# Four-layer convolutional network on one Trainium2 core: image additions moved to GpSimd and fills, stores and products reordered at two job boundaries

## The chip, the core and the metric

The kernel runs on one NeuronCore of a Trainium2 chip. The core has a matrix engine (TensorE, "PE" in the profile; its weight loads are listed apart as "PEld"), three engines for elementwise work (VectorE "DVE", ScalarE "ACT", GpSimd "POOL"), and SyncE ("SP"), which here only issues transfers. Each engine works through its own instructions in the order in which they were recorded, and waits on semaphores for the others. A transfer (DMA) is issued from a queue: SyncE's and ScalarE's go through a hardware queue each (q1 and q10 in the profile), GpSimd's through a software queue (q0). Matrix products are accumulated in PSUM banks; everything else lives in on-chip SBUF tiles or in DRAM.

The metric is the device time of one execution in microseconds (us), lower is better. One execution of each kernel is also recorded by the profiler; its trace starts at 0 and its length is called the span.

## What is computed

An image of 1024 channels by 64 x 64 pixels (4096 tokens) goes through four layers, each normalized in 32 groups and added back to its input:

```python
x = x + _L0_conv_ref(_gn(x), ...)   # decayed cumulative sum over the channels
x = x + _L1_conv_ref(_gn(x), ...)   # 1x1 convolution: einsum('oi,nihw->nohw', weight, x) + bias
x = x + _L2_conv_ref(_gn(x), ...)   # in_proj (three parts), scan over a permuted token order, out_proj
x = x + _L3_conv_ref(_gn(x), ...)   # 1x1 convolution + bias
return x
...
# the end of layer 2
y = y * jax.nn.silu(gate) + res
return jax.nn.silu(jnp.einsum('oc,bchw->bohw', out_proj_w, y) + out_proj_b[None, :, None, None])
...
def _gn(v, G=32, eps=1e-5):
    g = v.reshape(B_, G, C_ // G, H_, W_)
    m = jnp.mean(g, axis=(2, 3, 4), keepdims=True)
    s = jnp.var(g, axis=(2, 3, 4), keepdims=True)
    return ((g - m) / jnp.sqrt(s + eps)).reshape(v.shape)
```

Every large part is a 1024 x 1024 matrix times a 1024 x 4096 image. Layer 3 can only start once layer 2's whole output is known, since its normalization needs the mean and variance of each group of channels over all 4096 pixels. A group lies inside one block of 128 channels, so that the upper 512 channels (row 0) and the lower 512 (row 1) can be normalized one after the other.

## The kernel before

**Jobs.** The last 1070 us of the span belong to `two_steps` (line 1514). It works through twelve jobs: for each of four pairs of 512-pixel column blocks a "gate" job (third part of in_proj) and an "out" job (out_proj), then four "last" jobs (layer 3). Jobs are counted from 0: job 7 is the last out_proj job, job 8 the first of layer 3 (`turning`). Each job multiplies a 1024 x 1024 matrix by a 1024 x 1024 piece of the image with Strassen's scheme (in Winograd's form) applied twice. On the outer level the piece is four tiles b11, b12 (row 0, left and right columns) and b21, b22 (row 1), each 128 partitions x 4 sub-tiles (k = 0 to 3) x 512 columns, and four sums of them:

- t1 = b12 - b11, t2 = b22 - t1, t3 = t2 - b11, t4 = b21 - t2.

There are seven outer products, P1 (b11), P2 (b21), P3 (b22), P4 (t4), P5 (t1), P6 (t2), P7 (t3), and inside each the same seven again, on quarters of the outer operand. I write P5P2 for the inner product P2 of the outer product P5. The 49 products of a job are 8 matmuls each (128 x 256 columns), with a weight tile of 256 KB that SyncE loads ten tiles ahead (`wq`). P1P1, P1P2 and P1P3 read quarters of b11 itself: P1P1 its sub-tiles k = 0, 1, the other two k = 2, 3. P1P6, P1P7, P1P5 and P1P4 read the inner sums t2, t3, t1 and t4 of b11, which `inner_sum` (line 1547 is the subtraction) makes on GpSimd.

**Where work stands.** `plan(j)` puts every other instruction of a job at a slot: `then(slot, f)` appends it to `at[slot]`; a slot stands behind one product. The loop at the end of `two_steps` goes through the slots: first the product, then the slot's list in the order in which it was planned. So what an engine does, and in which order, is fixed by hand. Products of two outer products are interleaved: even places of a slot group of seven take P1, P2, P6, P7 of the current outer product, odd places P5, P4, P3 of the one before. At the first slots of job 8 a table (`instead`) puts the three leftovers of job 7 first.

**The names that matter here.**

- `fetch` (L1544) loads a 1 MB tile (`x_x_b11` and so on, or the image `x_x_D`, `x_x_Q`, `x_x_V` that is added back) on ScalarE's queue; `fill` (L1551) normalizes one sub-tile on ScalarE into `qb`; `comb` makes an outer sum (t1 overwrites b12, by `alias`) on VectorE, through the same line 1547.
- `emit` empties a product's PSUM bank: a "put" into a fresh tile is a ScalarE copy (L1752), anything else a VectorE sum (L1754 to L1763). A later product that adds onto the same bank waits for that.
- The out_proj job has four result tiles, C, D, Q and V, each 128 x 4 x 512. In job 7 (`final`, so `quick`) each sub-tile takes silu (L1715, ScalarE), the addition of the image (L1717, VectorE), and `quarter_stats` (L1590, VectorE bn_stats); then `keep` (L1729) stores the tile to `x2_d` on ScalarE's queue.
- `next_norm` makes layer 3's normalization, for row 0 from slot 44 of job 7 and for row 1 from slot 56 (that is slot 7 of job 8): `gn_mv` (L183, the statistics summed on VectorE), the small matmul `pg` (L200), `gn_d` (L203 to L205, VectorE), the small matmul `pv` (L209), `gn_v`, then logarithm and exponential on ScalarE (L170, L171) and four VectorE steps to `gn_bias` (L220). The ScalarE functions logarithm and silu need different tables: a table load stands where it changes (L1598, and at L1715).
- At the start of job 0 the last results of the stage before are still coming: `activate` (L1095 silu, L1097 store to `res_d`) empties the list `silus`; before the loop ends this is called with GpSimd as the issuing queue, and two tiles (`rg`) are left for it.

Of the kernel before, what the change touches and what calls it, by code (L numbers as in the profile page):

```python
# [15 lines left out]
ALU = mybir.AluOpType  # L16
# [78 lines left out]
def tile_net(ctx: ExitStack, tc: tile.TileContext, x, par_d, cst_d, w_d, w2_d, dbcw_d, out):  # L95
# [1266 lines left out]
    with tc.tile_pool(name="l2g", bufs=8) as pgat, tc.tile_pool(name="l2b", bufs=2) as pb, tc.tile_pool(name="l2r2", bufs=4) as prg, tc.tile_pool(name="l2h", bufs=1) as ph, \  # L1362
# [87 lines left out]
        with tc.manual_schedule(engines={E_.DVE, E_.PE, E_.Pool, E_.Activation}):  # L1450
            for k in range(5):
                gather(k)
            while given < first:
                next_units(total)
                if len(silus) > 3:
                    activate(4)
            step_sums(0)
            for k in range(-1, NK + 1):
                upto = first + (k + 2) * (total - first) // (NK + 2)
                if 4 < k + 5 < NK:  # L1460
                    gather(k + 5)
                turned = turn_rows(k + 1) if k + 1 < NK else None
                if k > 0:
                    weigh(k - 1, pgs.pop(k - 1))
                if turned is not None:
                    spread_decay(k + 1, *turned)
                if k + 2 < NK:
                    step_sums(k + 2)
                next_units(upto)
                y = apply(k - 1) if k > 0 else None  # L1470
                if 0 <= k < NK:
                    pgs[k] = cross(k)
                if k + 1 < NK:
                    nc.scalar.activation(decay_[k + 1], decay_[k + 1], AF.Exp)
                if y is not None:
                    scatter(k - 1, y)
                next_units(upto)
                if given // 2 % 14 != 12:
                    next(sums, None)
                if len(silus) > 3:  # L1480
                    activate(4)
            while given < total:
                next_units(total)
            next(units, None)
            while silus:
                activate(4, nc.gpsimd)
            for _ in sums:
                pass
    rg_pool.__exit__(None, None, None)
# [24 lines left out]
    def two_steps(jobs, norm2):  # L1514
# [3 lines left out]
        orders = [ORDER_B if kind == "out" else ORDER_A for kind in kinds]  # L1518
        orders[turning - 1 : turning + 1] = ORDER_C, ORDER_D
        norm3 = {}  # L1520
        at = {}
        held = {}
        inner = {}
        bank = {}
# [66 lines left out]

        def next_norm(s0):

            for row, slot, after, last in ((0, 44, (4, 4, 5, 5), 5), (1, 56, (3, 3, 4, 4), 5)):
                steps = {}

                def begin(row=row, steps=steps):
# [13 lines left out]
        def plan(j):  # L1611
# [6 lines left out]
            def on(slot, f, *a):  # L1618
                then(s0 + slot, lambda: f(*a))


            if kind != "out":
                for name, row, col, slot, when in (
                        (("b11", 0, 0, -7, 1), ("b12", 0, 1, -3, 2), ("b21", 1, 0, 6, 12), ("b22", 1, 1, 8, 14))
                        if order is ORDER_D else
                        (("b11", 0, 0, -25, -14), ("b12", 0, 1, -14, -3), ("b21", 1, 0, -10, -1), ("b22", 1, 1, 1, 8))):
                    on(slot, fetch, src_d, pair, row, col, (j, "x", name))
                    for k in range(KH):
                        on(when + (k // 2 if when in (1, 12) and order is ORDER_D else k), fill, j, name, row, col, k)
                late = [(1, "t1", "b12", "b11"), (9, "t2", "b22", "t1"), (13, "t3", "t2", "b11"), (27, "t4", "b21", "t2")]  # L1630
                ks = [range(KH)] * 4
                put_in = {2: 12}
# [6 lines left out]
                put_in = {1: 4, 3: 19}  # L1639
            if order is ORDER_C:  # L1640
                late[3] = (32, *late[3][1:])
            for (slot, to, a, b), kk in zip(late, ks):
                for i, k in enumerate(kk):
                    on(slot + i, comb, j, to, a, b, k)

            def alias(to, old):
                held[j, to] = tile_of(j, old)
            at[s0 + late[0][0]].insert(0, lambda: alias("t1", "b12"))
            at[s0 + late[2][0]].insert(0, lambda: alias("t3", "b11"))
            if order is not ORDER_D:  # L1650
                at[s0 + late[3][0]].insert(0, lambda: alias("t4", "b22" if order is ORDER_C else "t2"))
# [49 lines left out]
            for name, row, col, when in done:  # L1701
# [4 lines left out]
                for k, slot in when.items():  # L1706
                    o = row * KH + k

                    def one(name=name, nb=nb, row=row, k=k, o=o):
# [4 lines left out]
                            return  # L1714
                        nc.scalar.activation(c, c, AF.Silu, bias=pcol("bout", o))  # L1715
                        if quick:
                            nc.vector.tensor_tensor(c, c, held[j, "x", name][:, k], ALU.add)  # L1717
                            quarter_stats(tile_of(j, name), row, nb, k)
                    on(slot, one)
                    if kind == "last":  # L1720
# [12 lines left out]
                if not quick:  # L1733
# [3 lines left out]
                            on(when[k + 1] + 10 + i, lambda name=name, row=row, nb=nb, k=k + i: quarter_stats(  # L1737
                                tile_of(j, name), row, nb, k))
                    end += 11
                on(end + 1, keep)  # L1740
            if kind == "out" and final:
                next_norm(s0)

# [21 lines left out]
        def product(j, outer, name):  # L1765
# [15 lines left out]
            for o in range(OG):  # L1781
                for k in range(2):
                    nc.tensor.matmul(ps[:, o, :], w[:, k, o * P : (o + 1) * P], rhs[:, k, :],  # L1783
                                     start=(new and o == 0 and k == 0), stop=(k == 1), skip_group_check=True)
            for kind, row, col in {"P1": [("put", 0, 0)], "P2": [("add", 0, 0)], "P6": [("put", 1, 0)],
                                   "P7": [("put", 1, 1)], "P5": [("put", 0, 1), ("add", 1, 1)],
                                   "P4": [("add", 1, 0)], "P3": [("add", 0, 1)]}[name]:
                emit(j, outer, kind, row, col, ps)

        for j in range(len(jobs)):  # L1790
            plan(j)
        end = len(jobs) * JOB
# [3 lines left out]
        for slot in range(min(at), max(max(at), end + 6) + 1):  # L1796
# [3 lines left out]
            if 0 <= step < 7 * len(jobs):  # L1800
                j, s = divmod(step, 7)
                outer = orders[j][s]
                product(j, outer, ("P1", "P5", "P2", "P4", "P6", "P3", "P7")[i])
            for f in at.get(slot, ()):
                f()

    with tc.manual_schedule(engines={E_.DVE, E_.PE, E_.Pool, E_.Activation}):
# [101 lines left out]
```

## Time and profile before

| | |
|---|---|
| time, median of 3 runs | 2644.04 us |
| fastest, slowest of them | 2640.99, 2644.49 us |
| the profiled execution | 2645.31 us |
| its span | 2643.2 us |
| granted TensorE clock, mean | 0.994 of full |
| TensorE busy | 2559.3 us (97%) |
| VectorE, GpSimd, ScalarE busy | 1818.2 (69%), 1212.4 (46%), 1057.0 (40%) |
| moved by DMA | 597.22 MB, mean 226 GB/s |

Busy time is the sum over an engine's instructions. With TensorE at 97% of the span, what another engine does counts only where TensorE waits for it. In timelines a line reads: start, length, engine, source line, operation, output from inputs, shapes, count, and in brackets how long the engine was idle before it and what ended that. In the chain of waits each line is a piece of work that the next one had to wait for. Line numbers are those of the kernel before; in the kernel after, lines up to 1617 keep their numbers and later ones stand 6 to 13 lines further down (the matmuls of the products at L1793, the image addition at L1727).

### The profile page before, as it was taken

Reading aid. Unit: us, or ns where it says so; the run is one execution under the profiler, and the core shown is the slowest. Engines: PE = TensorE matmul, PEld = TensorE weight load, DVE = VectorE, ACT = ScalarE, POOL = GpSimd, SP = SyncE. Lnnn points to the kernel's source line nnn. Section 1 sums busy time; section 2 is a strip of 40 time slices with the busy share of each in tenths; the row PEclk is TensorE's granted clock in tenths of the full one; section 3 lists DMA queues with packets and bytes.
Section 4 is the critical chain, followed back from the end, with each engine's and each line's share of the span. In section 5 each row is a group of like instructions: output and inputs, shape, how many; then the busy total and the mean of one; then the engine's idle time right before and its main releaser. Section 6 shows DMA issues by size and latency. Waiting matters only on the chain.

```text
span 2643.2 us, 30741 instructions
## 1 busy us (share of the span) xinstructions
PE 2559.3 (97%) x9588; PEld 1712.5 (65%) x9588; DVE 1818.2 (69%) x3782; ACT 1057.0 (40%) x1799; POOL 1212.4 (46%) x1098
## 2 busy tenths in 40 slices
PE   5889999999999999999999999999999999899999
PEld 5764444444555445544454558888888888788887
DVE  7987675665564554377877766576585775877877
ACT  4672010005655644476867662233233322312120
POOL 2553223322414241256464645566565755554544
PEclk9999999999999999999999999999999999999999
DMA  6565648655655676577677847899898898888896
GB/s 253 189 211 170 232 137 284 209 158 189 196 147 139 151 193 158 178 248 224 206 241 241 282 140 209 223 281 290 237 298 254 240 303 224 277 287 301 301 320 216
DMA packets 426868, 597.22 MB, mean 226 GB/s; under 512 B 142004, under 2 KB 210739, under 8 KB 423636
## 3 DMA queue, kind: packets, MB, share of 16 engines
q1 hardware_dynamic: 307268, 384.68, 46.1%
q10 hardware_dynamic: 91456, 136.33, 14.7%
q0 software_dynamic: 27984, 74.26, 11.8%
q8 instruction: 78, 1.28, 0.2%
q14 instruction: 82, 0.67, 0.1%
HBM read 435.10 MB, written 160.05 MB: 225 GB/s over the span
## 4 chain that ended last, share of the span: by engine, by line
PE 83%; DVE 9%; ACT 5%; issue 1%; DMA 1%; POOL 1%; SPq 0%; DVEq 0%; POOLq 0%; ACTq 0%
PE mm L892 37%; PE q_P2P L1783 6%; PE q_P6P L1783 5%; PE q_P5P L1783 5%; PE q_P3P L1783 5%; PE q_P7P L1783 5%; PE q_P4P L1783 5%; PE q_P1P L1783 5%; PE py L1430 2%; PE l2pt L1145 2%; DVE xt L658 1%; DVE cvp L1126 1%; ACT b L996 1%; PE pd L623 1%; DVE stats L567 1%
## 5 line engine op out<-in xcount | busy, mean ns | idle before, releaser
L892 PE MATMUL mm<-t,w 128*128 128x512 f32 x1536 | 681.1, 594 | 0.0
L892 PE MATMUL mm<-b,w 128*128 128x512 f32 x1152 | 512.7, 596 | 5.0 <-ACT b L996 3.9
L892 PEld LDWEIGHTS mm<-t,w 128*128 128x128 f32 x1536 | 285.8, 190 | 321.3 <-issue 314.3
L892 PEld LDWEIGHTS mm<-b,w 128*128 128x128 f32 x1152 | 215.3, 191 | 252.0 <-issue 239.1
L1439 POOL DMA_INDIRECT y_rows<-g,dst x74 | 74.1, 1002 | 185.0 <-ACT g L1435 171.3
L1126 DVE SCALAR_TENSOR_TENSOR cvp<-xs,par,cvp 128x512 f32<-128x512 f32 x128 | 95.3, 753 | 76.8 <-ACT cvp L1123 74.5
L1752 ACT COPY qQ<-q_P5P 128x512 f32<-128x512 f32 x48 | 28.1, 585 | 292.0 <-PE q_P5P L1783 292.0
L470 POOL TENSOR_TENSOR s<-s 128x256 f32<-128x256 f32 (+3 forms) x120 | 130.3, 1091 | 7.5
L1433 ACT COPY g<-py 8x512 f32<-8x512 f32 x146 | 83.8, 574 | 107.5 <-PE py L1430 103.3
L1177 DVE TENSOR_TENSOR xs<-mm,xs 128x512 f32<-128x512 f32 x64 | 41.8, 685 | 116.1 <-PE mm L892 116.1
L1153 POOL TENSOR_TENSOR acc<-l2xt,acc 128x136 f32<-128x136 f32 x56 | 27.8, 497 | 194.4 <-ACT l2xt L1147 187.3
L1013 DVE SCALAR_TENSOR_TENSOR image<-mm,par,image 128x512 f32<-128x512 f32 x64 | 47.2, 746 | 89.8 <-PE mm L892 89.8
L1145 PEld LDWEIGHTS l2pt<-both,cv 128*128 128x128 f32 x512 | 76.1, 190 | 37.8 <-issue 21.5
L850 POOL TENSOR_TENSOR t<-t,b 128x512 f32<-128x512 f32 x40 | 55.7, 1419 | 88.6 <-DVE t L850 85.2
L996 ACT ACTIVATE b<-image,gnl_bias,gnl_r_r 128x512 f32<-128x512 f32 x48 | 36.9, 807 | 144.0 <-PE mm L892 116.7
L1551 ACT ACTIVATE qb<-x_x_b,gn_bias,gn_r_r 128x512 f32<-128x512 f32 x64 | 48.8, 807 | 113.8 <-DVE qQ L1713 49.2
L1783 PE MATMUL q_P4P<-t_t,wq_P4P 128*128 128x256 f32 x384 | 92.3, 384 | 1.3 <-DVE qV L1760 1.3
L1783 PE MATMUL q_P1P<-t_b,wq_P1P 128*128 128x256 f32 x384 | 92.2, 385 | 1.5 <-POOL t_b L1547 1.5
L1547 POOL TENSOR_TENSOR t_t<-qt 128x512 f32<-128x512 f32 x23 | 29.6, 1289 | 136.1 <-DVE qt L1547 76.5
L1760 DVE TENSOR_TENSOR qV<-q_P4P,qV 128x512 f32<-128x512 f32 x96 | 64.8, 686 | 38.6 <-PE q_P4P L1783 36.9
L1783 PE MATMUL q_P5P<-t_t,wq_P5P 128*128 128x256 f32 x384 | 90.8, 379 | 0.0
L1783 PE MATMUL q_P6P<-t_t,wq_P6P 128*128 128x256 f32 x384 | 90.7, 379 | 0.0
(432 smaller groups left out, 5953.9 us busy)
## 6 DMA issues: line engine op xcount, KB each, us to landing
w<-s_d SPq DMA_DIRECT2D x96, 512.0 KB
w<-in_w_dram SPq DMA_DIRECT2D x72, 512.0 KB
x_x_b<-x_d ACTq DMA_DIRECT2D x28, 1024.0 KB
image<-x_d SPq DMA_DIRECT2D x12, 2048.0 KB
wq_P6P<-s_d SPq DMA_DIRECT2D x84, 256.0 KB
wq_P7P<-s_d SPq DMA_DIRECT2D x84, 256.0 KB
wq_P5P<-s_d SPq DMA_DIRECT2D x84, 256.0 KB
wq_P3P<-s_d SPq DMA_DIRECT2D x84, 256.0 KB
```

Of the source, the lines that this page charges most:

```text
L470: eng.tensor_tensor(out, a, b, ALU.subtract)
L850: eng.tensor_tensor(B[name][k], B[one][k], B[two][k], ALU.subtract)
L892: nc.tensor.matmul(to[o], w[:, k, o * P : (o + 1) * P], B[name][k], start=(fresh and k == 0), stop=(k == KH - 1), skip_group_check=True)
L996: nc.scalar.activation(t, X[nb][:, ct, :], AF.Identity, bias=bias, scale=scale)
L1126: nc.vector.scalar_tensor_tensor(cv, xo[:, at + t : at + t + FB], pcol("dww", 3 * o + t), cv, ALU.mult, ALU.add)
L1145: nc.tensor.matmul(pt[:, q * NV : (q + 1) * NV], cv[:, (q0 + q) * P : (q0 + q + 1) * P], both[:, o, :], start=True, stop=True)
L1430: nc.tensor.matmul(py, G2[k % 2], rows[k][:, :DH], start=True, stop=True)
L1433: nc.scalar.copy(rows[k + 1][h * LC : h * LC + S, :DH], py[h * LC : h * LC + S])
L1439: nc.gpsimd.indirect_dma_start(out=y_views[k % len(y_views)][:, :], out_offset=bass.IndirectOffsetOnAxis(ap=dst_[:, k : k + 1], axis=0), i ...
L1551: nc.scalar.activation(tile_of(j, name)[:, k], held[j, "x", name][:, k], AF.Identity, bias=bias, scale=scale)
L1760: nc.vector.tensor_tensor(to, ps, to, ALU.add)
L1783: nc.tensor.matmul(ps[:, o, :], w[:, k, o * P : (o + 1) * P], rhs[:, k, :], start=(new and o == 0 and k == 0), stop=(k == 1), skip_group_c ...
```

## The change

- The two last stores of `res_d` are issued from ScalarE's queue instead of GpSimd's.
- The outer product P1 of job 0, and that of job 8, take their inner products in another order: P1, P2, P3, P6 at the even places and P7, P5, P4 at the odd ones (before: P1, P2, P6, P7 and P5, P4, P3). P3's bank is then emptied by a "put" and P5's by an "add".
- In job 8 the fills of row 0 (b11 and b12) and the combs of t1 stand ahead of everything else that is planned for the same slot (`early`).
- In job 7 the image is added on GpSimd for all of V and for two of the four sub-tiles of D; the rest stays on VectorE.
- In job 7 the store of Q is planned two slots later.
- Row 1's normalization takes its first small matmul a slot later, and so the steps behind it.

```diff
@@ the end of the stage before
             while silus:
-                activate(4, nc.gpsimd)
+                activate(4, nc.scalar)
@@ two_steps
-        at = {}
+        at, early = {}, {}
@@ next_norm
-            for row, slot, after, last in ((0, 44, (4, 4, 5, 5), 5), (1, 56, (3, 3, 4, 4), 5)):
+            for row, slot, after, last in ((0, 44, (4, 4, 5, 5), 5), (1, 56, (4, 4, 5, 5), 5)):
@@ plan
+            def ahead(slot, f, *a):
+                if order is ORDER_D:
+                    early.setdefault(s0 + slot, []).append(lambda: f(*a))
+                else:
+                    on(slot, f, *a)
...
                     for k in range(KH):
-                        on(when + (k // 2 if when in (1, 12) and order is ORDER_D else k), fill, j, name, row, col, k)
+                        (ahead if row == 0 else on)(when + (k // 2 if when in (1, 12) and order is ORDER_D else k),
+                                                    fill, j, name, row, col, k)
...
+            def alias(to, old):
+                held[j, to] = tile_of(j, old)
+            if order is ORDER_D:
+                ahead(late[0][0], alias, "t1", "b12")
             for (slot, to, a, b), kk in zip(late, ks):
                 for i, k in enumerate(kk):
-                    on(slot + i, comb, j, to, a, b, k)
-
-            def alias(to, old):
-                held[j, to] = tile_of(j, old)
-            at[s0 + late[0][0]].insert(0, lambda: alias("t1", "b12"))
+                    (ahead if to == "t1" else on)(slot + i, comb, j, to, a, b, k)
+            if order is not ORDER_D:
+                at[s0 + late[0][0]].insert(0, lambda: alias("t1", "b12"))
...
                         nc.scalar.activation(c, c, AF.Silu, bias=pcol("bout", o))
                         if quick:
-                            nc.vector.tensor_tensor(c, c, held[j, "x", name][:, k], ALU.add)
+                            eng = nc.gpsimd if name == "V" or (name == "D" and k < 2) else nc.vector
+                            eng.tensor_tensor(c, c, held[j, "x", name][:, k], ALU.add)
                             quarter_stats(tile_of(j, name), row, nb, k)
...
-                on(end + 1, keep)
+                on(end + (3 if final and name == "Q" else 1), keep)
@@ product
+            first, second = ("add", "put") if (j, outer) in starts else ("put", "add")
             for kind, row, col in {"P1": [("put", 0, 0)], "P2": [("add", 0, 0)], "P6": [("put", 1, 0)],
-                                   "P7": [("put", 1, 1)], "P5": [("put", 0, 1), ("add", 1, 1)],
-                                   "P4": [("add", 1, 0)], "P3": [("add", 0, 1)]}[name]:
+                                   "P7": [("put", 1, 1)], "P5": [(first, 0, 1), ("add", 1, 1)],
+                                   "P4": [("add", 1, 0)], "P3": [(second, 0, 1)]}[name]:
                 emit(j, outer, kind, row, col, ps)
@@ the loop over the slots
+        starts = {(0, orders[0][0]), (turning, orders[turning][0])}
...
-                product(j, outer, ("P1", "P5", "P2", "P4", "P6", "P3", "P7")[i])
-            for f in at.get(slot, ()):
+                product(j, outer, (("P1", "P7", "P2", "P5", "P3", "P4", "P6") if (j, outer) in starts else
+                                   ("P1", "P5", "P2", "P4", "P6", "P3", "P7"))[i])
+            for f in early.get(slot, []) + at.get(slot, []):
                 f()
```

The number of instructions on each engine changes by the six additions and the two stores alone.

## The prediction

> **What bounds the kernel now.** I read the run's stretches first: busy time of each engine, then the TensorE clock (1.00 is full), the share of the DMA engines and GB/s.
>
> ```profile
> core 0: us, PE busy (x) PEld busy (x) DVE busy (x) ACT busy (x) POOL busy (x), PEclk, DMA share, GB/s
> 1573.00:1589.00 16.00, 12.97 (x57) 10.51 (x57) 7.11 (x8) 11.44 (x18) 12.27 (x10) 1.00 0.47 138
> 1589.00:2276.80 687.80, 687.80 (x3314) 605.58 (x3312) 470.11 (x650) 198.66 (x312) 419.22 (x317) 1.00 0.89 259
> 2276.80:2318.00 41.20, 32.95 (x126) 25.49 (x126) 29.76 (x60) 19.44 (x32) 12.10 (x9) 0.88 0.78 255
> 2318.00:2600.00 282.00, 282.00 (x1308) 248.07 (x1307) 214.70 (x291) 52.78 (x76) 149.03 (x106) 1.00 0.87 294
> ```
>
> TensorE is the bound at full clock from 1589 to 2276.8 and from 2318 to 2600; nothing off it counts there. It is idle in two places only, and the edits touch just these: the entry of the 49-product jobs (3.0 us idle) and the turn from the last out_proj job (7) to layer 3 (8.3 us idle, and a mean clock of 0.88). A product (8 matmuls) takes 1.73 us at full clock. From 2276.80 to the first P2 product at 2316.68 run 14 products, 24.2 us of work in 39.9: 15.7 us are lost, and that is the most the turn can give. Next, the chain of waits through the turn (start, length, what):
>
> ```profile
> 2276.50 0.69 DVE stats L1590
> 2277.20 0.96 DVE gn_mv L183 x4
> ...
> 2279.21 0.69 DVE qV L1760
> ...
> 2279.95 3.46 PE q_P4P L1783 x8
> ...
> 2286.08 1.52 ACT qb L1551 x2
> ...
> 2287.62 1.28 ACT L1715
> ...
> 2289.64 2.12 ACT qb L1551 x3
> ...
> 2303.64 0.60 DVE qb L1547
> ...
> 2304.28 2.93 PE q_P5P L1783 x6
> ```
>
> It runs through DVE, whose order is strict: the first norm's sums (gn_mv) wait for the last qD sums; P4P5 at 2279.95 waits for DVE to add up its bank; the comb of qb12 that P5P2 needs ends at 2304.2, behind image additions and statistics; the lower norm reaches qb21 at 2315.81 and P2P1 at 2316.68, 30.6 us after the first fill at 2286.08, which I call zero. Both eight-matmul groups behind the long gaps ran at half speed: 2279.95 took 3.3 us, and 14 matmuls from 2304.28 took 6.0.
>
> Last, timelines: two image additions on VectorE, with GpSimd busy and idle; one GpSimd operation alone and one beside VectorE.
>
> ```profile
> 2292.93 1.76 DVE L1717 TENSOR_TENSOR qQ<-qQ,x_x_Q 128x512 f32<-128x512 f32 x1
> 2298.99 0.67 DVE L1717 TENSOR_TENSOR qV<-qV,x_x_V 128x512 f32<-128x512 f32 x1
> ```
>
> ```profile
> 2291.19 1.27 POOL L1547 TENSOR_TENSOR t_b<-qb,t_b 128x512 f32<-128x512 f32 x1 [2.25 <-ACT qb L1551]
> 2294.11 1.72 POOL L1547 TENSOR_TENSOR t_b<-qb,t_b 128x512 f32<-128x512 f32 x1
> ```
>
> So an addition costs VectorE 0.67 alone and up to 1.76 in company; on GpSimd it is 1.27 to 1.72, and GpSimd is idle for 15.69 us before 2287.68 and for 6.57 before 2304.37.
>
> **Entry, about 1573.** The third product was P1P6, started 1580.39. The profile names GpSimd as its releaser, but the operand t2 was done at 1578.40; P1P6 adds onto P1P1's bank, which ScalarE copied out from 1579.73 to 1580.29. I take that copy as the releaser. Now P1P3, which needs only filled rows, comes third: 1.73 us of work for a 1.46 us gap. Against it: the two res_d stores leave GpSimd's queue (0.60 and 0.56 there) for ScalarE's, ahead of the second fill. The second store waits for the silu ending 1574.88; an issue on ScalarE's queue takes 0.37 to 0.41 in the timeline; so the fill moves from 1574.79 to 1575.32, +0.53, and so does P1P1's second half. It hides nothing on GpSimd: its first t sum began 1575.77, after the fill of 1575.59. Then 22 matmuls at 0.216 run from 1576.17 to 1580.92, and the copy, 0.53 later too, frees the bank at 1580.82. P2P1, P1P7 and P2P2 find their operands done. Eighth product: before 1589.10, now 1587.8. Gain **1.3** (1.9 if the issues hide, 0.5 if the stores delay the fill by 1.3). SP only swaps P1P3's weight load with P1P7's. TensorE being the bound up to the turn, the gain is kept.
>
> **Turn, up to the first fill.** In this paragraph and the next I use the old times, without the 1.3. Two of the four qD additions leave VectorE, 0.68 each. GpSimd is free at 2271.99 and, the silus being done at 2271.67, adds until 2274.5 (2 x 1.26: VectorE then reads PSUM). VectorE does the two statistics in between and begins the sums at 2275.75, not 2277.11: 1.35 sooner. P4P5 then starts at 2278.6, and TensorE's gap shrinks from 3.15 to 1.8 us. If it stays at full clock, P4P5 ends at 2280.35 and the variance matmul (pv) no longer waits for it but for gn_d, 2280.85; VectorE's two sums of P4P5 end at 2282.05; the norm's end needs 1.44 (2284.64 to 2286.08 before). First fill 2283.45: gain **2.6**. At half clock P4P5 would end 1.6 later and the gain be 1.5. A gap of 1.46 at 1578.93 left the clock at 1.00 and one of 3.15 did not; 1.8 is nearer to the first, so I take 2.6. The qD store and b12's fetch move up 1.9 with it. The fetch must now be landed at 2286.25 instead of 2290.95; the DMA engines were full till 2284 and at 134 GB/s from 2286, the weights alone, so it lands about 2285.
>
> **Turn, from the first fill to P2P1** (us after the fill). ScalarE: five fills to 3.5 (before, the table load cut in after two), table load 1.28, then silus (0.62), fills (0.70) and copies (0.46) in turn. The fills of qb12 are out at 3.6, 6.8, 8.1, 10.5 (before 5.7, 7.5, 9.4, 11.8), qV's first silu at 9.3. The qQ store, which blocked ScalarE for 3.67 us at 2298.4 till VectorE's addition, now follows the fetch of b21, both last silus and the table load: gone. VectorE sheds four qV additions (0.67 to 1.03, 3.1 in all); its last comb, behind two contended operations of some 1.2 each, ends about 14.3 (before 18.2). TensorE: P1P1, P1P2, P1P3, P1P6 to 8.1, P5P1 to 9.9.
>
> Here the new wait stands. GpSimd's order puts qV's first addition, which waits for the silu at 9.3, ahead of t3, ready at 4.2 (before, done at 8.1). Both contended by VectorE's next comb, the addition and t3 end about 12.5, and P1P7 starts then: a gap of 2.6. P5P2 follows at 14.3, P1P5 to 17.7. GpSimd makes seven operations from 9.35 to t2 of qb12's comb: 8.8 us alone, 11.8 all contended; four of them meet two-input work on VectorE, so 7 x 1.25 + 4 x 0.4 = 10.3, done 19.6; P5P6 waits 1.8 for it. Its last addition ends 20.9, statistics and sums 22.6, pg (now behind P5P6), three VectorE sums of 0.6, gn_d 0.55, pv, one sum, 1.44 for the norm's end: qb21 at 27.0, P2P1 at 27.85 instead of 30.6. Gain **2.75**; GpSimd's bounds move P2P1 between 26.3 and 29.4, so 1.2 to 4.3. All 11 products before P2P1 are the same set, so this is TensorE's whole gain.
>
> Sum: 1.3 + 2.6 + 2.75 = 6.7 us. The profiled execution took 2645.31, span 2643.2, so 2.1 lie around it; it becomes 2638.6 with a span of 2636.5. It is 1.27 above the median shown, 2644.04; from that, **2637.3**.
>
> The gap of 2.6 raises the clock again. In the row, a stretch with 0.67 us of work between idle 1.36 and 2.53 still lost the clock (0.50 from 2304 to 2310). The Trainium skill (TensorE: Matmul & The Clock Gate, Part 1) drops it after an idle window of about 3.4 us, free-running; by this rule a gap of 2.6 costs nothing, and the sum stays 6.7. Reading the row the other way, P1P7 and P5P2 at half speed end 3.4 later, of which the 1.8 wait for t2 absorbs half: the sum would be about 5.
>
> **Rivals.** (a) GpSimd takes VectorE's place: its operations all contended (P2P1 at 29.4, gain 1.2), the clock halved in the first gap (1.5) and the stores hardly hidden (0.5): 3.2 us, 2640.8. For it: two of the new waits are GpSimd's. Against it: VectorE has few two-input operations after 15.4. The Trainium skill (GPSIMD Engine Reference, Engine selection and Key points) speaks for this rival: it keeps such additions on VectorE, about twice as fast, and lets the two contend where a VectorE instruction has two SBUF inputs; by that rule alone the gain would be these 3.2. The rows agree on the factor (0.67 against 1.27).
> (b) Slower: layer 3's b22 comes late. Its fetch stands on ScalarE's queue behind the qV store, which waits for GpSimd until 20.9, and the qQ store issued about 16. ScalarE needs it for the fill at 30.5, and bank copies are queued behind that fill. Over 2200 to 2330 ScalarE's DMA queue moved 14.67 MB in 130 us, 113 GB/s; at that share the 3 MB (3.15e6 bytes) take 27.9 us from 16, landing at 43.9, 13.4 late. Were TensorE stopped for all of it, 6.7 less 13.4: 2650.7. It decides from a landing after 37.2. Against it: before, two such stores and two fetches issued from 2301.6 were gone when the DMA rate fell to 229 and then 52 GB/s at 2316 to 2320, 15.7 us for 4 MB; at that rate the last 2 MB, from 21.2, land about 29.
> (c) The turn's gain goes to another wait and only the entry's 1.3 stays: 2642.7. Against it: the chain shows no third engine with work behind VectorE.
>
> **Chances and range.** Forecast 0.68 (its own range 2632.5 to 2638.7), (a) 0.17, (b) 0.10, (c) 0.05. About 0.2% (5.3 us) is what a measurement can tell from no change: faster 0.68; same 0.22, from (a) and (c); slower 0.10. The low end adds the bounds 1.9, 2.6 and 4.3 to 8.8 and takes the fastest run shown into account (2640.99): 2632. The high end reaches over (a) and (c): 2643.5.
>
> **What would show it.** Right: P1P3 third at the entry with no gap over 1 us before P1P6; gn_mv some 1.3 us sooner against P4P7's end; five fills in a row before the table load; no ScalarE wait at the qQ store; P2P1 28 us after the first fill; TensorE waiting for GpSimd's t3 and t2. Wrong: a half clock at P4P5; a fill of qb12 or qb22 ended by a DMA; P2P1 at 30 us or later; a wait at the rg stores that is longer than 0.6 us.

## The result, and the profile after

The changed kernel takes 2636.34 us (median of 12 runs, 2634.30 to 2640.25) against 2642.90 us (12 runs, 2638.78 to 2647.24) for the kernel before on the same chip: a ratio of 0.9976, 95% interval 0.9968 to 0.9985, that is 4.0 to 8.5 us less. The profiled execution took 2638.49 us, its span 2636.4.

The busy time by stretches, in the columns shown before, each boundary taken at the same work of the kernel:

```profile
core 0: us, PE busy (x) PEld busy (x) DVE busy (x) ACT busy (x) POOL busy (x), PEclk, DMA share, GB/s
1571.00:1587.20 16.20, 14.13 (x57) 11.87 (x58) 7.24 (x7) 11.66 (x18) 11.07 (x8) 0.89 0.47 135
1587.20:2273.80 686.60, 686.17 (x3305) 604.12 (x3304) 470.29 (x648) 198.59 (x312) 421.88 (x319) 1.00 0.89 259
2273.80:2312.00 38.20, 32.14 (x137) 25.61 (x137) 28.85 (x57) 20.02 (x33) 17.82 (x13) 0.96 0.81 288
2312.00:2594.00 282.00, 282.00 (x1308) 248.26 (x1307) 216.56 (x292) 52.01 (x75) 147.87 (x106) 1.00 0.88 295
```

The turn (third row) has GpSimd at work for 17.82 us and a mean clock of 0.96 instead of 0.88. The entry (first row) has less idle time but a mean clock of only 0.89, where it was 1.00. So one of the two places got better and the other did not, in this execution.

The chain of waits through the turn (start, length, what):

```profile
2274.52 0.96 DVE gn_mv L183 x4
...
2282.04 3.63 ACT qb L1551 x5
2285.69 1.28 ACT L1724
...
2291.51 1.27 POOL qV L1727
2292.78 1.13 POOL t_b L1547
...
2301.94 1.24 POOL qV L1727
2303.20 0.69 DVE stats L1590
...
2309.22 0.82 ACT qb L1551
```

It still goes from the upper norm's sums to the lower norm's fill, but from 2291.51 to 2303.18 it now runs through GpSimd. In the kernel before, the same part of the chain ran through VectorE's additions and combs:

```profile
2291.78 1.22 DVE qb L1547
2293.01 1.70 DVE qQ L1717
...
2302.31 0.60 DVE qV L1717
```

Five fills now stand in a row ahead of the table load. TensorE's own lines of the same stretch:

```profile
2275.57 0.35 PE L200 MATMUL gn_pg<-gn_mv,cst 128*128 128x4 f32 x2
2277.28 1.99 PE L1793 MATMUL q_P4P<-t_t,wq_P4P 128*128 128x256 f32 x8 [1.35 <-DVE qV L1770]
...
2294.50 3.37 PE L1793 MATMUL q_P1P<-t_b,wq_P1P 128*128 128x256 f32 x8 [2.40 <-POOL t_b L1547]
...
2301.99 1.99 PE L1793 MATMUL q_P5P<-t_t,wq_P5P 128*128 128x256 f32 x8 [0.35 <-POOL t_t L1547]
2304.91 0.38 PE L200 MATMUL gn_pg<-gn_mv,cst 128*128 128x4 f32 x2 [0.93 <-DVE gn_mv L183]
...
2310.09 2.27 PE L1793 MATMUL q_P2P<-qb,wq_P2P 128*128 128x256 f32 x8 [0.77 <-ACT qb L1551]
```

P4P5 at 2277.28 runs at full clock (1.99 instead of 3.46 us). P1P7 waits 2.40 us for GpSimd's t3 and then runs at half speed (3.37). P2P1 comes 28.05 us after the first fill (2282.04), before it was 30.60.

**Where the 6.8 us of span between the two profiled executions come from.** Four stretches, each from one start on TensorE or ScalarE to another: the first product began 2.43 us sooner (1571.85 against 1574.28). The stage before it is already 2.42 ahead at its last table load (1564.84 against 1567.26), where no instruction differs yet, and over 13 profiles of thirteen kernels the first product lies anywhere from 1569.42 to 1574.54, so this part is not the change. The entry, from the first product to the eighth's start, took 15.34 instead of 14.82: 0.52 lost. The long middle took 0.69 more, 0.4 of it in one wait for a weight tile. The turn, from P4P7's start to P2P1's, took 36.25 instead of 41.62: 5.37 gained. The rest is 0.2.

So the time from the first product to the end of the span is the cleaner measure of one profile: 1068.9 before, 1064.6 after, 4.4 us less. The table below uses it.

### The profile page after: what moved, and what is told of

It reads as the page before. It is cut to its first block, busy times and chain, and to the rows that moved or that the text cites. A ratio compares the mean times of both kernels' runs of the same rounds, so it can differ in the third digit from the quotient of the medians.

```text
span 2636.4 us, 30737 instructions
## 1 busy us (share of the span) xinstructions
PE 2556.5 (97%) x9588; PEld 1712.0 (65%) x9588; DVE 1820.3 (69%) x3776; ACT 1057.4 (40%) x1799; POOL 1218.7 (46%) x1102
## 4 chain that ended last, share of the span: by engine, by line
PE 51%; DVE 3%; ACT 3%; DMA 1%; issue 1%; POOL 1%; SPq 0%; DVEq 0%; ACTq 0%
PE mm L892 10%; PE q_P3P L1793 5%; PE q_P2P L1793 5%; PE q_P1P L1793 5%; PE q_P4P L1793 5%; PE q_P5P L1793 5%; PE q_P7P L1793 5%; PE q_P6P L1793 5%; PE py L1430 2%; PE pr L1391 1%; DMA wq_P6P<-s_d 1%; ACT b L996 1%; PE pg L1413 1%; ACT g L1433 0%; PE pr L1392 0%
```

## The experiments

Eleven kernels, all variants of the changed one, and their diffs are against it. "Entry": first product to the eighth's start. "Up to fill": P4P7's end (its start plus 1.73) to the first fill. "From fill": first fill to P2P1. "Turn": P4P7's start to P2P1's. "To end": first product to the end of the span. All in us of the profiled execution; the last column is the ratio of times to the kernel before, on the same chip in the same session, with its 95% interval.

| kernel | entry | up to fill | from fill | turn | to end | ratio to before |
|---|---|---|---|---|---|---|
| before | 14.82 | 9.29 | 30.60 | 41.62 | 1068.9 | 1 |
| after | 15.34 | 6.47 | 28.05 | 36.25 | 1064.6 | 0.9976 (0.9968 to 0.9985) |
| e1_entry_only | 13.67 | 7.94 | 30.56 | 40.23 | 1066.2 | 0.9997 (0.9988 to 1.0006) |
| e2_entry_pool | 13.15 | 6.48 | 28.35 | 36.56 | 1062.2 | 0.9978 (0.9969 to 0.9987) |
| e3_image_vector | 13.68 | 7.94 | 26.58 | 36.25 | 1062.3 | 0.9986 (0.9977 to 0.9995) |
| e4_d_only | 15.34 | 6.47 | 28.59 | 36.79 | 1064.4 | 0.9979 (0.9970 to 0.9988) |
| e5_no_early | 13.66 | 6.46 | 30.57 | 38.76 | 1064.7 | 0.9989 (0.9980 to 0.9998) |
| e6_q_store_back | 13.66 | 6.48 | 29.61 | 37.82 | 1063.8 | 0.9990 (0.9981 to 0.9999) |
| e7_sums_first | 13.66 | 6.47 | 26.21 | 34.41 | 1060.4 | 0.9971 (0.9959 to 0.9984) |
| e8_p1_first | 13.14 | 6.45 | 26.51 | 34.69 | 1060.3 | 0.9968 (0.9955 to 0.9980) |
| e9_pool_sums | 13.15 | 6.48 | 26.42 | 34.63 | 1060.3 | 0.9972 (0.9959 to 0.9984) |
| e10_norm_back | 15.34 | 6.48 | 31.19 | 39.40 | 1067.4 | 0.9998 (0.9989 to 1.0007) |
| e11_old_order | 15.34 | 6.48 | 29.69 | 37.90 | 1065.6 | 0.9989 (0.9980 to 0.9998) |

By time only e1 and e10 can be told from the changed kernel: the intervals of all others meet its own. What follows on single edits therefore rests on one profile of each kernel. The same code gave turns of 36.25 and 36.56 (after, e2) and of 34.41 and 34.63 (e7, e9), so differences of 0.3 us in this column mean nothing.

### The entry alone

The kernel before with the two edits of the entry: stores on ScalarE's queue, new order of job 0's first outer product.

```diff
-        starts = {(0, orders[0][0]), (turning, orders[turning][0])}
+        starts = {(0, orders[0][0])}
```

and four more edits taken back: the additions on GpSimd, the early fills, the store of Q and the norm's slot, which follow one by one below.

> The kernel before with the entry's two edits alone (the two res_d stores on ScalarE's queue, P1's new order in job 0). Measures: the entry is the time from the first P1P1 matmul to the start of the eighth product (before 14.8 us, after 15.3); the turn is the time from the start of P4P7, the product ahead of the norm's first small matmul, to the start of P2P1 of job 8 (before 41.6, after 36.3). Theory: the order removes the 1.46 us gap and the stores cost 0.5, so the entry is 13.5 us where the clock stays at 1.00 and 15.3 where it is 0.50 for 3.4 us, as in the profile after; turn 41.6; total 0 to 1.3 us under before. Rival (the entry carries part of the gain): total more than 3 us under before, turn unchanged.

The entry took 13.67, that is 1.15 less than before, at full clock; the turn's stretch from the fill is the old one (30.56). The turn as a whole is 1.39 shorter than in the profile before, and 1.35 of that is P4P5, which ran at full clock here behind the same wait (more on this below). Over all runs the time is no different from before that could be told (0.9997). Two lines each of TensorE's timeline, first of the kernel before, with its gap of 1.46 ahead of the third product:

```profile
1575.64 3.29 PE L1783 MATMUL q_P1P<-qb,wq_P1P 128*128 128x256 f32 x14 [0.70 <-ACT qb L1551]
1580.39 3.69 PE L1783 MATMUL q_P1P<-t_b,wq_P1P 128*128 128x256 f32 x16 [1.46 <-POOL t_b L1547]
```

Now those of this kernel, where the gap is gone:

```profile
1570.57 0.67 PE L1793 MATMUL q_P1P<-qb,wq_P1P 128*128 128x256 f32 x2 [0.88 <-DVE rg L1089]
1572.46 5.02 PE L1793 MATMUL q_P1P<-qb,wq_P1P 128*128 128x256 f32 x22 [1.22 <-ACT qb L1551]
```

Then those of the changed kernel, whose code is the same here:

```profile
1571.85 0.67 PE L1793 MATMUL q_P1P<-qb,wq_P1P 128*128 128x256 f32 x2 [0.88 <-DVE rg L1089]
1573.74 6.70 PE L1793 MATMUL q_P1P<-qb,wq_P1P 128*128 128x256 f32 x22 [1.22 <-ACT qb L1551]
```

The same 22 matmuls behind the same idle times (0.88, 0.67 of work, 1.22) took 5.02 us in one and 6.70 in the other, where the granted clock over 1574.80 to 1578.20 was 0.51. Of the nine profiles with the stores on ScalarE's queue four show the entry of 15.34 and five that of 13.66 to 13.68.

The clock records of the traces show what decides. At the entry and the turn half clock lasts 3.41 or 6.83 us, and it always starts on a fixed grid of 3.41 us (in the changed kernel at 1574.75 and at 2294.96, which is 211 such steps later). It follows a step in which TensorE was busy for less than half of the time. Two steps of the changed kernel, then two of e1, in the columns of the stretches above (TensorE's busy time stands behind the first comma, the clock is the third number from the end):

```profile
1571.34:1574.75 3.41, 1.68 (x7) 1.21 (x8) 0.36 (x1) 2.60 (x4) 0.98 (x1) 1.00 0.48 184
1574.75:1578.16 3.41, 3.41 (x10) 2.70 (x9) 1.21 (x1) 3.41 (x6) 3.14 (x4) 0.50 0.29 77
```

```profile
1570.10:1573.51 3.41, 1.72 (x7) 1.24 (x8) 0.32 (x1) 2.64 (x4) 1.02 (x1) 1.00 0.47 180
1573.51:1576.92 3.41, 3.41 (x18) 3.00 (x17) 1.22 (x1) 3.41 (x6) 3.14 (x4) 1.00 0.36 82
```

Half of 3.41 is 1.71: 1.68 lost the clock, 1.72 kept it. Between 210 us and the last few us of the span half clock sets in 16 times in the 13 traces, each time behind a step that was 17 to 49% busy. Of some 9,000 other steps at full clock only one was less than 49.5% busy (44%, in e7). So two things decide: where the idle times fall on this grid, which no edit here sets, and how much of one step they can fill.

### The stores back on GpSimd's queue

```diff
-                activate(4, nc.scalar)
+                activate(4, nc.gpsimd)
```

> The kernel after with the two res_d stores back on GpSimd's queue. Theory: the second fill comes 0.5 us sooner, the gaps ahead of P1P1's second half shrink from 2.1 us to 1.6 in all as they were before, the clock stays at 1.00; entry 13.0 us, turn 36.3, total 0.5 to 2.3 us under the kernel after. Rival (the stores had to leave GpSimd, whose t sums are late behind them): entry 14 us or more with TensorE waiting for t2 or t3 of b11, total at or above the kernel after.

The entry took 13.15, another 0.52 less: TensorE's second idle time in it is 0.70 instead of 1.22, as in the kernel before. In the three profiles with this edit (e2, e8, e9) the entry is 13.14 to 13.15 and the clock stays full. So in the profiles the move of the stores only costs: 0.52 each time, and 1.67 more where the clock halves. That risk came with it: idle times of 0.88 and 1.22 in one step of 3.41 us leave it 38% busy, 0.88 and 0.70 leave it 54% busy, which is above the half (the lowest in these profiles are 39 and 54%). By time the gain cannot be told (0.9978 beside 0.9976 for the changed kernel).

### All image additions on VectorE

```diff
-                            eng = nc.gpsimd if name == "V" or (name == "D" and k < 2) else nc.vector
+                            eng = nc.vector
```

> The kernel after with all image additions of job 7 back on VectorE; the early fills, the late store, the norm's slot and the order of the products stay. Theory of the prediction (the additions of D make the first fill sooner, those of V relieve VectorE's queue): first fill 9.3 us after P4P7's end as before (after: 6.5), P2P1 29 to 30 us after the first fill, turn 40 to 41. Rival (the additions of V only move the wait from VectorE to GpSimd, and the early fills and the late store give the second half of the gain): first fill 9.3 as well, but P2P1 24.5 to 26 us after it, since t3 and t2 of qb12's comb no longer stand behind the silus and VectorE's sums end at 19 us instead of 22.6; turn 35.5 to 37, total within 1 us of the kernel after.

The theory, a turn of 40 to 41, fails; the rival's 35.5 to 37 holds. Up to the first fill 1.47 us were lost (7.94), from the fill to P2P1 1.47 were gained (26.58), and the turn is 36.25 in both. So in these two profiles the edit that the title names first, images added by GpSimd, is worth nothing in the turn as a whole: the first fill comes sooner by it, but P2P1 does not. By time it can't be told from the changed kernel (0.9986, interval 0.9977 to 0.9995). The stretch from the fill is still 4.0 us shorter than that of e1, so other edits must give that.

### Only D's additions on GpSimd

```diff
-                            eng = nc.gpsimd if name == "V" or (name == "D" and k < 2) else nc.vector
+                            eng = nc.gpsimd if name == "D" and k < 2 else nc.vector
```

> The kernel after with V's four image additions back on VectorE and D's two left on GpSimd. Theory of the prediction (GpSimd relieves VectorE): first fill 6.5 us after P4P7's end, P2P1 29 to 30 us after it, turn 37 to 38, total 1 to 2 us above the kernel after. Rival (V on GpSimd is a loss): P1P7 starts without a gap, P2P1 24.5 us after the first fill, turn 32.7, total 3.5 us under the kernel after and 9 to 10 under before.

28.59 is just below what the theory gave and far from the rival's 24.5; the turn is 36.79. The sooner fill and the shorter stretch behind it did not add. With the first fill sooner, b12 was not yet there, and later VectorE was late; ScalarE's line and three of TensorE's:

```profile
2284.56 0.81 ACT L1551 ACTIVATE qb<-x_x_b,gn_bias,gn_r_r 128x512 f32<-128x512 f32 x1 [1.15 <-DMA x_x_b<-x_d]
```

```profile
2295.53 1.56 PE L1793 MATMUL q_P5P<-qb,wq_P5P 128*128 128x256 f32 x6 [1.70 <-DVE qb L1547]
...
2302.86 0.39 PE L200 MATMUL gn_pg<-gn_mv,cst 128*128 128x4 f32 x2 [2.31 <-DVE gn_mv L183]
2303.10 3.01 PE L1793 MATMUL q_P1P<-t_b,wq_P1P 128*128 128x256 f32 x8
```

The fill waited 1.15 us for its transfer, the last comb was late behind V's additions (1.70), the lower norm's sums too (2.31), and the product behind that wait ran at half speed. VectorE, which got V's four additions back, is the bound again. Beside the changed kernel (28.05), which has V's additions on GpSimd, this is 0.54 more: V's move alone is no loss there, and hardly a gain.

### Without the early fills and combs

```diff
-                if order is ORDER_D:
-                    early.setdefault(s0 + slot, []).append(lambda: f(*a))
+                if False:
+                    early.setdefault(s0 + slot, []).append(lambda: f(*a))
```

> The changed kernel with one part undone: the fills of layer 3's upper tiles, the name t1 and the combs of qb12 stand again behind the rest of their step, as before the change. All else is as in the changed kernel. Theory (GpSimd's queue and the lower norm set P2P1, and ScalarE finishes its silus at the same time in any order): first fill as in the changed kernel (6.5 after P4P7's end); the fills of b11 are cut by the table load again, so the comb that P5P2 needs ends some 2.5 us later, but the last image addition of qV still ends about where it did: first fill to P2P1 28.3 to 29.3 us against 28.05. Rival (the early fills and combs give most of the 4.0 us by which the stretch from the first fill shrank with all image additions on VectorE): 30.5 or more. Time: 0.3 to 1.3 us above the changed kernel by the theory, 2.5 or more by the rival.

The rival was right: 30.57, 2.5 more than the changed kernel. TensorE's lines:

```profile
2297.28 2.93 PE L1793 MATMUL q_P5P<-qb,wq_P5P 128*128 128x256 f32 x6 [3.85 <-DVE qb L1547]
2300.00 3.07 PE L1793 MATMUL q_P1P<-t_b,wq_P1P 128*128 128x256 f32 x8
```

The comb was late as the theory said, but it did not stay hidden: TensorE waited 3.85 us for it, and the 14 matmuls behind that took 5.63 us (2297.28 to 2302.91) where 3.0 are full speed. These 2.6 us, more than the wait itself, are the loss: at full clock the lower norm's pg would have stood at 22.9 us after the fill (an estimate: it started 25.5 after it), as it did in the changed kernel.

### The Q store at its old slot

```diff
-                on(end + (3 if final and name == "Q" else 1), keep)
+                on(end + 1, keep)
```

> The changed kernel with one part undone: the qQ store stands on ScalarE's queue one slot behind the last qQ silu again, not three. It waits for VectorE's last qQ addition, which ended 17.5 us after the first fill in the changed kernel, and two qV silus wait behind it. Theory: ScalarE stands for some 5 us at the store, the third qV silu starts at 17.9 instead of 12.2, GpSimd's third qV addition about 1.7 later than now, and all behind it too: first fill to P2P1 29.7 us (28.9 to 30.5) against 28.05, time 1.7 above the changed kernel. Rival (the late store gives most of the 4.0): 31 or more. Second rival (GpSimd's queue hides the store's wait altogether): 28.0 to 28.4.

29.61 against the 29.7 expected: ScalarE stood 5.70 us at the store, and everything on GpSimd behind the third qV addition came later. Its timeline shows also what waits next:

```profile
2295.44 0.72 ACT L1724 ACTIVATE qV<-qV,par 128x512 f32<-128x512 f32 x1 [5.70 <-DVE qQ L1727]
...
2312.21 0.82 ACT L1551 ACTIVATE qb<-x_x_b,gn_bias,gn_r_r 128x512 f32<-128x512 f32 x1 [2.79 <-DMA x_x_b<-x_d]
```

b22's fetch, which follows the stores on this queue, then landed 2.79 us after ScalarE was ready for it.

### The lower norm's steps at their old slot

```diff
-            for row, slot, after, last in ((0, 44, (4, 4, 5, 5), 5), (1, 56, (4, 4, 5, 5), 5)):
+            for row, slot, after, last in ((0, 44, (4, 4, 5, 5), 5), (1, 56, (3, 3, 4, 4), 5)):
```

> The changed kernel with one part undone: the lower norm's steps one slot sooner, as before the change, so that TensorE's pg stands ahead of P5P6. Theory (the later slot lets P5P6 run in the wait for the means): pg waits for gn_mv from P1P5's end to 33.1 us after P4P7's end less 2.3, that is about 22.9 after the first fill; P5P6, pv, P1P4 and P5P7 follow it and P2P1 starts at 28.8 at full clock, 30.5 if the wait of some 3 us halves it, against 28.05; time 0.7 to 2.4 above the changed kernel. Rival (the slot makes no difference, the norm's own steps are the chain): 27.9 to 28.3.

31.19, beyond the upper end expected, and the time is back at that of the kernel before (0.9998; its interval does not meet that of the changed kernel). With pg ahead of P5P6, TensorE waits at pg while P5P6 is ready:

```profile
2303.72 0.39 PE L200 MATMUL gn_pg<-gn_mv,cst 128*128 128x4 f32 x2 [3.25 <-DVE gn_mv L183]
2303.96 3.42 PE L1793 MATMUL q_P5P<-t_t,wq_P5P 128*128 128x256 f32 x8
```

P5P6's operand had been done at 2300.76. A wait of 3.25, and half speed after it. Of the edits undone one at a time this one, four digits in a table of slots, cost most in its profile, and it alone is told from the changed kernel by time.

### The old order of layer 3's first products

```diff
-        starts = {(0, orders[0][0]), (turning, orders[turning][0])}
+        starts = {(0, orders[0][0])}
```

> The changed kernel with one part undone: the old order of layer 3's first outer product (P1P6 third, P1P7 fourth), the entry's order kept new. Theory (the new order gives TensorE two products to run while GpSimd makes t3): TensorE waits for t3 from about 8 to 12.5 us after the first fill with only three of its eleven products done, not five, and gets back some 2 of these 3.5 us from the later waits (0.35 at P5P6, 0.93 at pg, 0.77 at P2P1): first fill to P2P1 28.8 to 30.5 against 28.05, time 0.7 to 2.4 above the changed kernel. Rival (the norm is the bound, the order is hidden): 28.0 to 28.4, time within 0.5.

29.69, as the theory said. TensorE had only three products to run before t3:

```profile
2288.39 1.96 PE L1793 MATMUL q_P1P<-t_b,wq_P1P 128*128 128x256 f32 x8 [1.35 <-issue]
2294.62 3.26 PE L1793 MATMUL q_P1P<-t_b,wq_P1P 128*128 128x256 f32 x8 [4.26 <-POOL t_b L1547]
```

### The inner sums ahead of V's additions

The first kernel here that goes beyond the change. GpSimd makes all four inner sums of b11 before it waits for V's first silu.

```diff
-                    put_in = {0: 2, 1: 5, 2: 13, 3: 19, 4: 24}
+                    put_in = {0: 1, 1: 5, 2: 13, 3: 19, 4: 24}
...
-                    on(put_in.get(s, 7 * s - 5) + i, inner_sum, j, SIDES[p][1], i)
+                    (ahead if s == 0 and order is ORDER_D else on)(put_in.get(s, 7 * s - 5) + i, inner_sum, j, SIDES[p][1], i)
```

> The changed kernel with one thing added: the four inner sums of layer 3's b11 (t1 to t4) stand on GpSimd's queue ahead of qV's image additions. In the changed kernel the first qV addition waited for its silu until 9.5 us after the first fill with t3 behind it, and TensorE waited 2.40 us for t3. Theory: t3 is done by 5 us after the first fill, P1P7 starts without a wait, and GpSimd has two operations (1.71 and 1.26) less behind the silu, so that its last qV addition ends about 2.9 us sooner: first fill to P2P1 25.4 us at full clock, 27.1 if the wait at P5P2 (for the comb on VectorE, some 3 to 4 us) halves the clock; time 1 to 2.6 below the changed kernel. Rival (VectorE's additions, statistics and combs are the bound, t3's wait only stood beside it): 27.5 to 28.5, time within 0.6 of the changed kernel.

26.21, between the theory's two numbers, but at full clock, where it gave 25.4. GpSimd's timeline, then a line of TensorE's:

```profile
2283.68 1.60 POOL L1547 TENSOR_TENSOR t_b<-t_b,qb 128x512 f32<-128x512 f32 x1
2285.24 1.27 POOL L1547 TENSOR_TENSOR t_b<-qb,t_b 128x512 f32<-128x512 f32 x1
2289.05 1.27 POOL L1727 TENSOR_TENSOR qV<-qV,x_x_V 128x512 f32<-128x512 f32 x1 [2.54 <-ACT qV L1724]
```

```profile
2294.56 1.56 PE L1793 MATMUL q_P5P<-qb,wq_P5P 128*128 128x256 f32 x6 [2.42 <-DVE qb L1547]
```

t3 is done 6.0 us after the first fill (2285.28 less 2279.26) instead of 12.4, and P1P7 does not wait. The last V addition ends at 19.3 instead of 21.1, 1.8 sooner and not the 2.9 expected, since two of GpSimd's operations took 1.72 and 1.73 beside VectorE's. Now the comb is what TensorE waits for (2.42), this time at full clock, though the step of the grid that holds most of this wait was busy for only 44%. With the sums first, the additions on GpSimd do pay: the turn is 34.41 (34.63 in e9) against 36.25 with all of them on VectorE (e3) and 36.79 with D's alone on GpSimd (e4). In those two t3 was done as soon, 6.0 and 5.7 us after the fill, since no addition stood ahead of it; part of e4's excess is the half clock seen there.

### P1's seven products first; sums and stores together

e8 has the early sums, the stores on GpSimd's queue and P1's products all ahead of P5's; e9 the first two alone.

```diff
+        instead.update({s3 + 7 + i: s3 + p for i, p in enumerate((8, 10, 12, 7, 9, 11))})
         for slot in range(min(at), max(max(at), end + 6) + 1):
```

> The same early inner sums, the res_d stores back on GpSimd's queue, and the seven products of P1, which need b11 alone, all ahead of P5's. Entry 13.15 us as in the run with only the stores put back. Theory: P1's seven products run without a gap from the first fill to 13.4 us after it, P5P2 finds its comb almost done, and the end is set by GpSimd's last qV addition and by VectorE's last statistics at about 19.5: first fill to P2P1 25.5 to 26.5 (four sums, 2.5 us, now stand between the norm's means and its differences, one more than before). Rival (VectorE's order costs what TensorE's order gains): 27.5 or more. Time: 2 to 3 us below the run with only the stores put back if the first holds, so about 2631.5 beside a kernel before of 2640.6.

> The changed kernel with the two edits that gained so far and nothing else: the two res_d stores back on GpSimd's queue, and the four inner sums of b11 ahead of qV's image additions. Theory (the two lie in different stretches and add): entry 13.15 us, P4P7 to P2P1 34.4, so 0.5 below the run with the early sums alone and 2.4 below the run with the stores alone: about 2632.5 beside a kernel before of 2641. Rival (the early sums' gain depends on the clock: the wait of 2.4 at P5P2 halves it in this run): turn 36, no better than the run with the stores alone.

e8's stretch from the fill is 26.51, no better than without the new order. The theory had its seven products run without a gap; they did not, since TensorE waited for a PSUM bank that ScalarE copies out only behind its silus:

```profile
2293.59 3.72 PE L1793 MATMUL q_P1P<-t_b,wq_P1P 128*128 128x256 f32 x16 [2.40 <-ACT qZ L1762]
```

In e9 entry and turn add as expected (13.15 and 34.63). By time e7, e8 and e9 are all faster than the kernel before (0.9971, 0.9968, 0.9972; medians 2633.97, 2632.82, 2634.45), and can't be told from each other or, by these intervals, from the changed kernel; from the first product to the end their profiles are 4.2 to 4.3 us shorter than that of the changed kernel. Not all of that is theirs: 0.69 is the changed kernel's long middle and 1.67 its half clock in the entry. The early sums give 1.6 to 1.8 of it, the stores 0.52.

## Why the prediction came true, step by step

**Total.** Forecast 2637.3 us and, for the profiled execution, 2638.6; measured 2636.34 and 2638.49. The second agreement is luck; its parts agree less well. In the pair of profiles the turn gave 5.37 (forecast 2.6 + 2.75 = 5.35), the entry lost 0.52 (forecast a gain of 1.3), the middle lost 0.69, and the earlier start of 2.43, which the change does not make, covered both. The medians of 12 runs each differ by 6.6 us, within an interval of 4.0 to 8.5.

**Entry, 1.3.** The mechanism is right and shown: P1P3 fills the gap, and the stores delay the second fill by 0.5 and P1P1's second half by 0.52. At full clock the gain is 1.15. What the step left out is the clock: it weighed gaps against the clock in the turn but not the 0.88 and 1.22 that stand here around 0.67 us of work. With half clock in four entries of nine the mean is (4 x 15.34 + 5 x 13.67) / 9 = 14.4, a gain of 0.4 in place of 1.3. That is below the lower bound of 0.5.

**Up to the first fill, 2.6.** Measured 2.82. The sums do start sooner, by 1.46 (forecast 1.35), and P4P5 keeps the full clock. e1 and e3 split it: with all additions on VectorE, but full clock at P4P5, the stretch is 7.94, so moving D's additions is worth 1.47 and the other 1.35 is the half clock that the profile before had there. The prediction took that half clock as given, but e1 and e3 have the same wait and kept the clock: their idle time straddled two steps of the grid (57% busy at the least); in the profile of the kernel before it fell into one (37%). So 1.35 of the 2.82 is luck of the profile that was taken first. What the change does is to shorten that gap to 1.35, which leaves a step 60% busy.

**From the fill to P2P1, 27.85.** Measured 28.05, and nearly every step on the way: P1P7's start at 12.5 (12.46), the gap ahead of it 2.6 (2.40), t2 of qb12's comb at 19.6 (19.89), GpSimd's seven operations 10.3 us (10.42), the last addition at 20.9 (21.1), qb21 at 27.0 (27.2). VectorE's last comb ended at 15.9, not 14.3, and P5P2 began 1.3 later than forecast, but P5P6 waited for GpSimd's t2 all the same. Wrong in it was that a gap of 2.6 costs the clock nothing: P1P7 ran at half speed. The alternative named there, a sum of about 5, is wrong too: P1P7 and P5P2 lost 1.8 us by the clock, but P5P6 was to wait 1.8 for GpSimd, and the wait shrank to 0.35. The rule of the Trainium skill (TensorE: Matmul & The Clock Gate, Part 1), a drop after an idle window of about 3.4 us that runs freely, fits the lengths and the grid: at both places, wherever one of the 13 profiles has half clock, it lasts 3.4 or 6.8 us. The window need not be idle throughout, though: less than half of work in it was enough. A gap of 2.40 us fell into one step in the changed kernel (30% busy) and lost the clock; in e8 a gap of 2.40 lay across two (77 and 53%) and kept it; the entry lost it with work inside the window.

**What the prediction did not see.** It put the gain from the fill on down to the additions that VectorE sheds, and counted the early fills, the later store and the norm's slot as parts of the same sum. Undone one at a time they cost 2.5 (e5), 1.6 (e6), 3.15 (e10) and, for the order of the products, 1.65 (e11), together 8.9, where the whole stretch gained 2.55. All additions back on VectorE made it 1.47 shorter and the way to the fill 1.47 longer (e3). So the prices do not add: with one edit missing, the others show little or nothing, and the price of an edit holds only beside the rest. And three of these prices contain half clock behind a wait of over 3 us, which took 2.6 us of TensorE's time in e5 and 1.7 each in e10 and e11.

**The rivals.** (a) GpSimd did take VectorE's place in the chain, but not at the price put on it: its operations took 1.26 to 1.72, and in the turn only P1P7 and the first of P5P2's matmuls met half clock. The rule cited with it, that such additions belong on VectorE (GPSIMD Engine Reference of the Trainium skill, Engine selection), is not borne out in the turn: in the order that the change gave them the additions cost nothing and gain nothing there (36.25 in both, e3), and with GpSimd's queue put in order they gain (34.41 against 36.25). The factor of about two in duration does hold (0.68 against 1.27). (b) shows in little: b22's tile was forecast to land 29 us after the fill and landed at 31.3, and its fill waited 0.72. That is one of the signs that the prediction named for being wrong, but TensorE lost nothing by it: from P2P1 to the end both kernels take some 326 us. e6 shows how near it is: 2.79, and 326 us still. (c) is refuted by the turn's 5.37.

## What to carry to other kernels

An addition moved to an idle engine is not free or dear by its duration, but by what stands behind it on that engine's queue: put what is ready ahead of what waits for another engine. Where TensorE idles in pieces of one to four microseconds, add up the idle time in any 3.4 us around a wait, price the wait with the clock behind it where that comes to more than half, and look whether a small matmul that must wait stands ahead of a product that need not. Compare kernels of which the end differs by a few microseconds stretch by stretch from a common point, since the same code ahead of it here varied by 5 us.

## What the runs showed of the hardware

- At the entry and the turn the granted clock halves for 3.41 or 6.83 us behind a step of a fixed 3.41 us grid in which TensorE was busy for less than half of the time (16 of 16 onsets in 13 traces: 17 to 49%; one step with 44% kept it). So idle times far below 3.4 us lose it or not by where they fall: 0.88 and 1.22 us around 0.67 us of work in four of nine profiles, 0.88 and 0.70 in none of four; a gap of 2.4 us in one kernel (after) and not in two (e7, e8).
- A store on ScalarE's queue that waits for ScalarE's own last result costs the activation behind it 0.5 us, though the issue itself takes 0.34: the second fill began 1.13 us after the silu's start instead of 0.63.
- VectorE and GpSimd slow each other: an addition or a comb on VectorE takes 0.68 alone and up to 1.74 to 1.78 beside one of GpSimd's, GpSimd's 1.27 becomes up to 1.72.
